# A Perceiver layer on one core: the order of ScalarE's operations bound to the order in which they are written, and four conversions spaced evenly

## The chip, the cores and the metric

The kernel runs on one core of a Trainium2 chip. A core has five engines that run side by side, each through its own queue in order: TensorE (PE in the profile; its weight loads are PEld), VectorE (DVE), ScalarE (ACT), GpSimd (POOL) and SyncE (SP), which here starts transfers. The metric is the device time of one launch in microseconds. Everything is in fp32.

## The reference

A layer of a Perceiver with 8 batches of 64 query rows of width 512 and a context of 1601 rows for each batch:

```
x = x + cross_attention(layernorm(x), context)   # 16 heads of 32, stablemax for softmax
x = x + self_attention(layernorm(x))             # 8 heads of 64, one key and value head, causal
x = x + ffn(layernorm(x))                        # 2 shared experts, and the best 2 of 8 experts

stablemax:  s = where(x >= 0, x + 1, 1 / (1 - x));  s / sum(s)
layernorm:  (x - mean) / sqrt(var + eps)
ffn experts: 512 -> 2048 -> 512, gelu between
```

The bulk of it is the projection of the 8 x 1601 context rows to keys and values, two 512 x 512 matrices.

## The kernel before

**Tiling.** The 512 query rows are four tiles of 128 (`NTT`). The context of one batch is three sections of 512 columns (24 in all) and a tail of 65 rows. Keys are kept transposed (`kT`), values by rows (`v`).

**Keys and values.** Section 0 is projected plainly (`first_keys` L383 on, `first_values`, `plain_values` L396 on): four key banks of PSUM, copied by ScalarE with the bias (L394), and one bank for each of four value products (copy in L400). From section 1 on, `products` (L337) uses a Strassen scheme: seven products of four matmuls for the keys and seven for the values of a section, in three PSUM banks that take turns (A, C, A, B, A, B, A). After product 0, 2, 3, 4 and 6 ScalarE copies the bank out (L344, or L348 twice with a bias for each half); after 1 and 5 VectorE adds. A product that takes a bank again needs the copy that reads it to be done. The sums of weight parts that the scheme needs are eight VectorE operations in `weight_parts` (L303), the differences of the context four GpSimd operations a section (L320).

**Attention.** A unit is two tiles of 128 keys of one batch, seven units a batch (the last is the tail). `score` (L504) fills four PSUM banks `ps_s` of 512 columns. `convert` (L525) turns one bank into stablemax's numerators: ScalarE writes relu(-s) (L535), relu(s) (L536) and adds 1 to the first (L537), VectorE takes the reciprocal (L538), GpSimd adds (L539) and, with every second conversion, adds to the running totals (L548, L551). The buffer `neg` is one of five. `weigh` (L555) multiplies with the values. `sums` and `finish` divide by the totals.

**First rows.** `first_rows` (L473) normalizes one tile of the queries: statistics on VectorE, `Norm.factors` (a square root on ScalarE, L258, then a reciprocal, L259, and a product, L261, on VectorE), `Norm.apply` on ScalarE (L266), four transposes on TensorE (L274) and the copy `xnT` on ScalarE (L275, in `transposed`). `q_unit` (L484) then makes the queries from all four tiles.

**Self attention.** For each pair of batches `chain` (L613) is a list of 15 steps (project, factors, apply, turn, keys, queries, scores, exps, flip, values, output, factors, apply2, rows, gate), spread over the next pair's work. Several of them end in one ScalarE operation.

**What sets the order.** The class `Plan` (L52) takes the TensorE work as units with lengths and everything else with due times, and writes the instructions in that order. A first-section product counts 3.43, a Strassen product 1.715; an attention unit of two tiles spans 11.77 of the plan's units (about 15.3 us on the chip), and its four conversions are due at 0, 0.3, 0.6 and 0.9 of it (L906). The first section's plan is: keys, first value product, the four `first_rows`, second value product, four `q_unit`, then the other value products. After writing, the framework's scheduler orders each engine's instructions itself, by what is ready and by its own costs: ScalarE's order in the kernel before is not the written one. So the four norms of the first rows stand ahead of the key copies in ScalarE's queue, though they are written after them; and at many places in the attention conversions stand ahead of a copy that is written before them.

**After the attention.** The experts follow. The first shared expert's first products (`first_hidden` L811, Gelu in L821) overlap with the last norm.

Of the kernel before, what the change touches and what calls it, by code (L numbers as in the profile page):

```python
# [1 line left out]

# [1 line left out]

# [67 lines left out]
            o[2]()  # L72


@with_exitstack
def perceiver_kernel(
    ctx: ExitStack,
# [4 lines left out]
    out,  # L82
):
    nc = tc.nc

    def pool(name, bufs, **kw):
        return ctx.enter_context(tc.tile_pool(name=name, bufs=bufs, **kw))
# [156 lines left out]
    class Norm:  # L244


        def __init__(self, tt):
            self.tt = tt
# [6 lines left out]

        def factors(self):
            self.rs = lnp.tile([P, 1], F32, name="ln_rs")
            nc.scalar.activation(self.rs, self.mv[:, 1:2], AF.Sqrt, bias=eps_t)  # L258
            nc.vector.reciprocal(self.rs, self.rs)  # L259
            self.nb = lnp.tile([P, 1], F32, name="ln_nb")  # L260
            nc.vector.scalar_tensor_tensor(  # L261
                self.nb, self.mv[:, 0:1], -1.0, self.rs, ALU.mult, ALU.mult
            )

        def apply(self, xn):
            nc.scalar.activation(  # L266
                xn, res[:, self.tt, :], AF.Identity, bias=self.nb, scale=self.rs
            )

    def transposed(dst, xn):  # L270

        pt = psx("pt").rearrange("p (c t) -> p c t", c=NC)
        for c in range(NC):
            nc.tensor.transpose(pt[:, c, :], xn[:, c * P : (c + 1) * P], ident)  # L274
        nc.scalar.copy(dst, pt)  # L275

    def cols(t):
        return t.rearrange("p (c t) -> p c t", c=NC)
# [1 line left out]
    plan = Plan()  # L280
# [56 lines left out]
    def products(i, keys):  # L337

        st = {}

        def copy(dst, src, half):

            if not keys or half is None:
                nc.scalar.copy(dst, src)  # L344
                return
            for k in range(2):
                g = 2 * half + k
                nc.scalar.activation(dst[:, k], src[:, k], AF.Identity, bias=bk_t[:, g : g + 1])  # L348

        def unit(n):  # L350
            bank, a, b = ORDER[n]
            if n == 0:
                t = w8("kT" if keys else "v")
                (kTs if keys else vs)[i] = t
                for f in range(2):
                    for r in range(2):
                        st[f, r] = t[:, 2 * f : 2 * f + 2, r * HF : (r + 1) * HF] if keys else \
                            t[:, 2 * r : 2 * r + 2, f * 256 : (f + 1) * 256]
            fresh = bank not in st
            if fresh:  # L360
                st[bank] = psa("ps_k" if keys else "ps_v").rearrange("p (k n) -> p k n", k=2)
            ps = st[bank]
            multiply(ps, (wkp if keys else wvp)[a], tparts[i][b], keys, first=fresh)
            if n == 0:
                copy(st[0, 0], ps, 0)
            elif n == 1:
                nc.vector.tensor_tensor(st[0, 0], ps, st[0, 0], ALU.add)
            elif n == 2:
                copy(st[0, 1], ps, 0)
            elif n == 3:  # L370
                copy(st[1, 1], ps, None)
            elif n == 4:
                u3 = snp.tile([P, 2, 256], F32, tag="sn", name="u3")
                copy(u3, ps, 1)
                nc.gpsimd.tensor_add(st[1, 1], st[1, 1], u3)
            elif n == 5:
                nc.vector.tensor_tensor(st[0, 1], ps, st[0, 1], ALU.add)
            else:
                copy(st[1, 0], ps, 1)

        return [lambda n=n: unit(n) for n in range(len(ORDER))]

    def first_keys():  # L383

        kTs[0] = w8("kT")
        ps = [psa("ps_k0") for _ in range(NG)]
        for c in range(NC):
            for g in range(NG):
                nc.tensor.matmul(  # L389
                    ps[g], wk[:, c, g * P : (g + 1) * P], cxs[0][:, c, :],  # L390
                    start=c == 0, stop=c == NC - 1,
                )
        for g in range(NG):
            nc.scalar.activation(kTs[0][:, g, :], ps[g], AF.Identity, bias=bk_t[:, g : g + 1])  # L394

    def plain_values(cx, dst, w):  # L396
        ps = psa("ps_v0")
        for c in range(NC):
            nc.tensor.matmul(ps[:w], cx[:, c, :], wv[:, c, :], start=c == 0, stop=c == NC - 1)  # L399
        nc.scalar.copy(dst, ps[:w])  # L400

    def first_values(t):
        if t == 0:
# [27 lines left out]
    def tail_keys(b):  # L431
        kT = tlp.tile([P, NG, 2, TAIL], F32, name="kTt")
        cx = tails[b, "x"]
        for g in range(NG):
            ps = psa("ps_kt")[:, : 2 * TAIL]
            for c in range(NC):
                nc.tensor.matmul(
                    ps, wk[:, c, g * P : (g + 1) * P], cx[:, c, :], start=c == 0, stop=c == NC - 1
                )
            for s in (slice(0, ROUND), slice(ROUND, TAIL)):  # L440
                nc.scalar.activation(
                    kT[:, g, :, s],
                    ps[:, 2 * s.start : 2 * s.stop].rearrange("p (k s) -> p k s", k=2),
                    AF.Identity, bias=bk_t[:, g : g + 1],
                )
        for k in range(2):
            tails[b + k, "k"] = kT[:, :, k, :]
# [3 lines left out]
    def tail_values(b):  # L451
        x = tails[b, "x"]
        ps = psa("ps_vt")
        for c in range(NC):
            nc.tensor.matmul(
                ps, x[:, c, 0 : 2 * ROUND], wv[:, c, :], start=c == 0, stop=c == NC - 1
            )
        for k in range(2):
            v = tails[b + k, "v"] = tlp.tile([P, E], F32, name="vt")
            nc.scalar.copy(v[:ROUND], ps[k * ROUND : (k + 1) * ROUND])  # L460
            nc.gpsimd.dma_start(out=v[ROUND:TAIL, :], in_=odd_v[b + k : b + k + 1, :])

    per = NSEC * SEC // P + 1
# [61 lines left out]
    def convert(b, u, j):  # L525

        w, n, k = tile_of(b, UNITS[u][0])[2], width(u), len(UNITS[u])
        r = j // 2
        if j % 2 == 0:
            attn[b, u, r] = at4("at")  # L530
        at = attn[b, u, r]
        pos = at[:w, (j % 2) * n : (j % 2 + 1) * n]
        ps = parts[b, u][j][:w].rearrange("p k g q -> p (k g q)")
        neg = np2("neg")[:w, :n]
        nc.scalar.activation(neg, ps, AF.Relu, scale=-1.0)  # L535
        nc.scalar.activation(pos, ps, AF.Relu)  # L536
        nc.scalar.activation(neg, neg, AF.Identity, bias=one_t[:w])  # L537
        nc.vector.reciprocal(neg, neg)  # L538
        nc.gpsimd.tensor_add(pos, pos, neg)  # L539
        if j % 2 == 0:  # L540
            return

        if u == 0 and r == 0:
            totals[b] = totp.tile([P, 2, 2, NG * SQ], F32, name="tot")
        tot = totals[b][:w, r]
        at = at[:w, : 2 * n].rearrange("p (j k c) -> p j k c", j=2, k=k)
        if u == 0:
            nc.gpsimd.tensor_add(tot, at[:, :, 0], at[:, :, 1])  # L548
        else:
            for i in range(k):  # L550
                nc.gpsimd.tensor_add(tot, tot, at[:, :, i])  # L551
# [3 lines left out]
    def weigh(b, u):  # L555
# [20 lines left out]
        if u == len(UNITS) - 1:  # L576
            acc = accs.pop(b)
            accs[b] = accp.tile([P, NG, SQ], F32, name="o_sb")
            nc.scalar.copy(accs[b], acc)

    ctT = {}

# [30 lines left out]
    def chain(tt):  # L613
# [35 lines left out]
        def keys():  # L649
# [12 lines left out]
                            skip_group_check=True,  # L662
                        )
            st["kv"] = qhp.tile([P, P], F32, name="akv")
            nc.scalar.copy(st["kv"], ps)

        def queries():
            ps = psx("ps_aq").rearrange("p (h q) -> p h q", h=H2)
# [7 lines left out]
                            skip_group_check=True,  # L676
                        )
            st["qh"] = qhp.tile([P, H2, SQ], F32, name="aqh")
            nc.scalar.mul(st["qh"], ps, float(E ** -0.5))
            st["wp"] = load_w(aWp, "awp")  # L680

        def scores():
# [22 lines left out]
        def exps():  # L705
            shape = [P, 2 * NP2, SQ]
            s = st["s"]
            nc.scalar.activation(s, s, AF.Exp)
            sm = lnp.tile([P, 2 * NP2, 1], F32, name="sm")
            nc.vector.tensor_reduce(sm, s, AX.X, ALU.add)  # L710
            nc.vector.reciprocal(sm, sm)
            nc.vector.tensor_tensor(s, s, sm.to_broadcast(shape), ALU.mult)

        def flip():
# [5 lines left out]
                        start=True, stop=True, skip_group_check=True,  # L720
                    )
            st["aT"] = sd("aT")
            nc.scalar.copy(st["aT"], pt.rearrange("p a r -> p (a r)"))

        def values():
            po = psx("po_a")
# [7 lines left out]
            st["oT"] = cols(sd("oT"))  # L734
            for half in halves:
                for j in range(2):
                    nc.scalar.copy(
                        st["oT"][j * HD2 : (j + 1) * HD2, :, half], po[half, :, j, :]
                    )

# [70 lines left out]
    def first_hidden(hc):  # L811
# [4 lines left out]
        for c in range(NC):  # L816
# [1 line left out]
                ps[:, :N0], w0[0, q][:, c, r * P : (r + 1) * P], shared_x["x"][:, c, :N0],  # L818
                start=c == 0, stop=c == NC - 1,
            )  # L820
        nc.scalar.activation(h0[q][:, r, :N0], ps[:, :N0], AF.Gelu, bias=b1_t[:, 0, hc : hc + 1])  # L821

    def first_second(hc):
        q, r = hc // QC, hc % QC
# [77 lines left out]
    for u, time in enumerate(when):  # L902
        plan.at(weighed[u], lambda u=u: weigh(*units[u]))
        plan.at(time, lambda u=u: begin(u))
        for j in range(1, 4):
            plan.at(time + 0.3 * j * wide[u] * step, lambda u=u, j=j: convert(*units[u], j))  # L906
        if u == 3 * nu:
            plan.at(time, clear)
    for tt in range(NTT):
# [614 lines left out]
```

## Time and profile before

| | us |
|---|---|
| median of 3 runs | 1389.02 |
| lowest, highest | 1387.26, 1390.02 |
| the profiled execution itself | 1385.32 |
| its span in the profile | 1383.6 |

Busy time by stages of that execution, from the table of windows:

| window (us) | TensorE | VectorE | ScalarE | GpSimd |
|---|---|---|---|---|
| 0 to 48: loads, first section | 42.56 | 19.89 | 11.09 | 23.02 |
| 48 to 150 | 102.00 | 92.63 | 67.51 | 80.54 |
| 150 to 857: attention | 695.27 | 641.33 | 445.83 | 583.10 |
| 857 to 1383.6: experts | 520.77 | 135.07 | 118.35 | 58.85 |

A row of the timeline gives start, duration, engine, line, operation, output and inputs, shapes and count, and in square brackets the idle time ahead of it with what ended it. A row of the waits gives the engine and line that waited, the engine and line that ended the wait, the sum in us, how many times, and the longest. Lines (L...) are those of the kernel before.

### The profile page before, as it was taken

The page shows a single profiled execution, that of the slowest core. Times are in us where ns is not written, and L with a number is a line of the kernel's source. Part 1 is how long each engine was busy: PE and PEld are TensorE (multiplying, and loading weights), DVE is VectorE, ACT ScalarE, POOL GpSimd, SP SyncE. Part 2 cuts the span into 40 slices and gives each one's busy share as a digit, 9 for nine tenths or more (in the row PEclk, how much of TensorE's full clock was granted, in tenths as well). Part 3 has the DMA queues.
Part 4 walks back from the last instruction along what each step waited for, and adds up shares of the span by engine and source line. Part 5 has one row for each costly group of instructions (what it writes and reads, how often), then busy time and mean ns, then how long its engine had stood idle before and what let it go on. Part 6 is the DMA issues. An engine that isn't in the chain of part 4 may idle for free.

```text
span 1383.6 us, 36463 instructions
## 1 busy us (share of the span) xinstructions
PE 1360.6 (98%) x16080; PEld 1073.2 (78%) x16080; DVE 888.9 (64%) x655; ACT 642.8 (46%) x1339; POOL 745.5 (54%) x672
## 2 busy tenths in 40 slices
PE   8999999999999999999999999999999999999998
PEld 3678788788788877778878878555786699977787
DVE  4698999988899997988988989713531000100314
ACT  3466656566666665666656766422221111122230
POOL 6288899886889986878979776600110000000020
PEclk9999999999999999999999999999999999999999
DMA  7002112112311121111111113444466267778730
GB/s 230 31 3 70 33 33 78 61 34 70 132 62 33 47 94 40 33 40 63 47 58 68 63 40 142 149 153 164 159 215 243 77 222 264 261 268 315 293 99 32
DMA packets 84804, 156.35 MB, mean 113 GB/s; under 512 B 13370, under 2 KB 14426, under 8 KB 84644
## 3 DMA queue, kind: packets, MB, share of 16 engines
q1 hardware_dynamic: 77732, 136.41, 28.3%
q0 software_dynamic: 4704, 13.91, 2.9%
q10 hardware_dynamic: 2208, 3.67, 0.9%
q8 instruction: 127, 2.08, 0.6%
q14 instruction: 33, 0.27, 0.1%
HBM read 143.24 MB, written 10.72 MB: 111 GB/s over the span
## 4 chain that ended last, share of the span: by engine, by line
PE 87%; ACT 4%; DVE 4%; POOL 3%; issue 2%; DMA 0%; DVEq 0%; POOLq 0%
PE ps_k L331 17%; PE ps_v L331 16%; PE ps_h L1367 11%; PE y L1312 6%; PE ps_s L520 4%; PE y L1321 4%; PE ps_hr L331 3%; PE ps_hh L331 3%; PE ps_o L570 3%; PE ps_h L817 3%; PE y L829 3%; DVE neg L538 3%; PE ps_v L399 1%; ACT neg L535 1%; PE ps_k L389 1%
## 5 line engine op out<-in xcount | busy, mean ns | idle before, releaser
L538 DVE RECIPROCAL neg<-neg 128x512 f32<-128x512 f32 (+1 forms) x224 | 683.8, 3091 | 57.8 <-ACT neg L537 54.6
L539 POOL TENSOR_TENSOR at<-at,neg 128x512 f32<-128x512 f32 (+1 forms) x224 | 266.6, 1195 | 126.2 <-DVE neg L538 123.2
L551 POOL TENSOR_TENSOR tot<-tot,at 128x512 f32<-128x512 f32 (+1 forms) x176 | 223.9, 1272 | 12.8
L1367 PEld LDWEIGHTS ps_h<-xgT,w1t 128*128 128x128 f32 x1024 | 147.2, 191 | 37.9 <-issue 32.7
L1372 ACT ACTIVATE hT<-ps_h,b1e 128x128 f32<-128x128 f32 (+4 forms) x128 | 50.3, 393 | 259.3 <-PE ps_h L1367 233.3
L537 ACT ACTIVATE neg<-neg,one_t 128x512 f32<-128x512 f32 (+1 forms) x224 | 162.1, 725 | 0.0
L1303 POOL DMA_DIRECT2D ys_d<-yo x12 | 6.6, 547 | 285.6 <-DVE yo L1302 285.6
L1367 PE MATMUL ps_h<-xgT,w1t 128*128 128x128 f32 (+4 forms) x1024 | 159.7, 299 | 0.0
L535 ACT ACTIVATE neg<-ps_s 128x512 f32<-128x512 f32 (+1 forms) x224 | 130.1, 583 | 62.8 <-PE ps_s L520 51.4
L331 PE MATMUL ps_k<-tx,sk 128*128 128x256 f32 x552 | 130.0, 386 | 3.8 <-ACT kT L348 3.6
L536 ACT ACTIVATE at<-ps_s 128x512 f32<-128x512 f32 (+1 forms) x224 | 131.7, 590 | 0.0
L331 PE MATMUL ps_v<-sv,tx 128*128 128x256 f32 x552 | 129.0, 384 | 1.0 <-ACT v L344 1.0
L331 PEld LDWEIGHTS ps_k<-tx,sk 128*128 128x128 f32 x552 | 101.5, 190 | 23.8 <-ACT kT L348 4.8
L331 PEld LDWEIGHTS ps_v<-sv,tx 128*128 128x128 f32 x552 | 102.4, 190 | 17.2 <-ACT v L344 1.4
L1294 DVE COPY xgT<-pt_x 128x512 f32<-128x512 f32 (+3 forms) x12 | 6.8, 592 | 141.0 <-PE pt_x L1293 141.0
L1312 PE MATMUL y<-w2t,hT 128*128 128x512 f32 x192 | 95.8, 593 | 0.0
L344 ACT COPY v<-ps_v 128x512 f32<-128x512 f32 x92 | 56.0, 608 | 75.0 <-PE ps_v L331 75.0
L348 ACT ACTIVATE kT<-ps_k,bk_t 128x256 f32<-128x256 f32 x138 | 59.5, 498 | 59.8 <-PE ps_k L331 59.8
L331 PE MATMUL ps_k<-cx,wk 128*128 128x256 f32 x368 | 86.8, 385 | 0.0
L331 PE MATMUL ps_v<-wv,cx 128*128 128x256 f32 x368 | 86.1, 383 | 0.0
L520 PEld LDWEIGHTS ps_s<-qT,kT 32*64 32x64 f32 x6144 | 69.9, 130 | 18.2 <-issue 16.8
L331 PEld LDWEIGHTS ps_k<-cx,wk 128*128 128x128 f32 x368 | 68.2, 190 | 12.8 <-issue 2.1
(263 smaller groups left out, 2013.1 us busy)
## 6 DMA issues: line engine op xcount, KB each, us to landing
w1t<-in_W_dram SPq DMA_DIRECT2D x32, 1024.0 KB, 11.5
w2t<-in_W_dram SPq DMA_DIRECT2D x32, 1024.0 KB, 12.2
cx<-in_ctxT_dram SPq DMA_DIRECT2D x23, 1024.0 KB, 5.4
w1t<-in_sW_dram SPq DMA_DIRECT2D x12, 1024.0 KB, 5.1
w2t<-in_sW_dram SPq DMA_DIRECT2D x12, 1024.0 KB, 5.6
wo<-in_woT_dram SPq DMA_DIRECT2D x4, 1024.0 KB, 5.5
awq<-in_aWq_dram SPq DMA_DIRECT2D x4, 1024.0 KB, 5.5
awp<-in_aWp_dram SPq DMA_DIRECT2D x4, 1024.0 KB, 5.6
```

Source lines behind the costliest of these rows:

```text
L331: nc.tensor.matmul(ps[:, k, :], l[:, c, k * P : (k + 1) * P], r[:, c, :], start=first and k == 0 and c == 0, stop=last and c == 1, skip_gr ...
L344: nc.scalar.copy(dst, src)
L348: nc.scalar.activation(dst[:, k], src[:, k], AF.Identity, bias=bk_t[:, g : g + 1])
L520: nc.tensor.matmul(ps[j][h, k, g, :], kT[rows, g, h], qT[rows, g, b * SQ : (b + 1) * SQ], start=True, stop=True, skip_group_check=True,)
L535: nc.scalar.activation(neg, ps, AF.Relu, scale=-1.0)
L536: nc.scalar.activation(pos, ps, AF.Relu)
L537: nc.scalar.activation(neg, neg, AF.Identity, bias=one_t[:w])
L538: nc.vector.reciprocal(neg, neg)
L539: nc.gpsimd.tensor_add(pos, pos, neg)
L551: nc.gpsimd.tensor_add(tot, tot, at[:, :, i])
L1312: nc.tensor.matmul(self.y[k], hT[:, s : s + w], w2t, start=first, stop=last)
L1367: nc.tensor.matmul(ph[:, : blk.n], w1t[:, c, f : f + P], blk.x[:, c, :], start=c == 0, stop=c == NC - 1,)
```

## The change

A class `InOrder` wraps an engine: each call through it is made under `tc.issue_after(...)` of the call before, so that the scheduler may not place it ahead of that one. `act = InOrder(tc, nc.scalar)` takes the place of `nc.scalar` for all ScalarE operations of the first rows, the products, the tails, the conversions, the self attention, the norms and the first shared expert's first Gelus. The other experts' operations, the gate's probabilities and the transfers started on ScalarE's queue are left free. Second, the four conversions of a unit are due at 0, 0.25, 0.5 and 0.75 of it. No operation is added or removed; the only new things are ordering constraints on one engine.

```diff
+class InOrder:
+    def __init__(self, tc, engine):
+        self.tc, self.engine, self.last = tc, engine, None
+
+    def __getattr__(self, name):
+        def ask(*args, **kw):
+            with self.tc.issue_after(self.last.ins) if self.last else nullcontext():
+                self.last = getattr(self.engine, name)(*args, **kw)
+            return self.last
+
+        return ask
...
+    act = InOrder(tc, nc.scalar)
...
         def factors(self):
-            nc.scalar.activation(self.rs, self.mv[:, 1:2], AF.Sqrt, bias=eps_t)
+            act.activation(self.rs, self.mv[:, 1:2], AF.Sqrt, bias=eps_t)
         def apply(self, xn):
-            nc.scalar.activation(
+            act.activation(
                 xn, res[:, self.tt, :], AF.Identity, bias=self.nb, scale=self.rs
             )
     def transposed(dst, xn):
-        nc.scalar.copy(dst, pt)
+        act.copy(dst, pt)
     def products(i, keys):
-                nc.scalar.copy(dst, src)
+                act.copy(dst, src)
-                nc.scalar.activation(dst[:, k], src[:, k], AF.Identity, bias=bk_t[:, g : g + 1])
+                act.activation(dst[:, k], src[:, k], AF.Identity, bias=bk_t[:, g : g + 1])
     def first_keys():
-            nc.scalar.activation(kTs[0][:, g, :], ps[g], AF.Identity, bias=bk_t[:, g : g + 1])
+            act.activation(kTs[0][:, g, :], ps[g], AF.Identity, bias=bk_t[:, g : g + 1])
     def plain_values(cx, dst, w):
-        nc.scalar.copy(dst, ps[:w])
+        act.copy(dst, ps[:w])
     def convert(b, u, j):
-        nc.scalar.activation(neg, ps, AF.Relu, scale=-1.0)
-        nc.scalar.activation(pos, ps, AF.Relu)
-        nc.scalar.activation(neg, neg, AF.Identity, bias=one_t[:w])
+        act.activation(neg, ps, AF.Relu, scale=-1.0)
+        act.activation(pos, ps, AF.Relu)
+        act.activation(neg, neg, AF.Identity, bias=one_t[:w])
...
-            plan.at(time + 0.3 * j * wide[u] * step, lambda u=u, j=j: convert(*units[u], j))
+            plan.at(time + 0.25 * j * wide[u] * step, lambda u=u, j=j: convert(*units[u], j))
```

The same replacement is made in `tail_keys`, `tail_values`, `weigh`, the self attention's `keys`, `queries`, `exps`, `flip`, `values`, and `first_hidden`.

More of the change, by code (lines that the diff above doesn't have):

```diff
@@ L1 @@
-from contextlib import ExitStack
+from contextlib import ExitStack, nullcontext
 import numpy as np
@@ L440, in tail_keys @@
             for s in (slice(0, ROUND), slice(ROUND, TAIL)):
-                nc.scalar.activation(
+                act.activation(
                     kT[:, g, :, s],
@@ L459, in tail_values @@
             v = tails[b + k, "v"] = tlp.tile([P, E], F32, name="vt")
-            nc.scalar.copy(v[:ROUND], ps[k * ROUND : (k + 1) * ROUND])
+            act.copy(v[:ROUND], ps[k * ROUND : (k + 1) * ROUND])
             nc.gpsimd.dma_start(out=v[ROUND:TAIL, :], in_=odd_v[b + k : b + k + 1, :])
@@ L578, in weigh @@
             accs[b] = accp.tile([P, NG, SQ], F32, name="o_sb")
-            nc.scalar.copy(accs[b], acc)
+            act.copy(accs[b], acc)
     ctT = {}
@@ L664, in keys @@
             st["kv"] = qhp.tile([P, P], F32, name="akv")
-            nc.scalar.copy(st["kv"], ps)
+            act.copy(st["kv"], ps)
         def queries():
@@ L678, in queries @@
             st["qh"] = qhp.tile([P, H2, SQ], F32, name="aqh")
-            nc.scalar.mul(st["qh"], ps, float(E ** -0.5))
+            act.mul(st["qh"], ps, float(E ** -0.5))
             st["wp"] = load_w(aWp, "awp")
@@ L707, in exps @@
             s = st["s"]
-            nc.scalar.activation(s, s, AF.Exp)
+            act.activation(s, s, AF.Exp)
             sm = lnp.tile([P, 2 * NP2, 1], F32, name="sm")
@@ L722, in flip @@
             st["aT"] = sd("aT")
-            nc.scalar.copy(st["aT"], pt.rearrange("p a r -> p (a r)"))
+            act.copy(st["aT"], pt.rearrange("p a r -> p (a r)"))
         def values():
@@ L736, in values @@
                 for j in range(2):
-                    nc.scalar.copy(
+                    act.copy(
                         st["oT"][j * HD2 : (j + 1) * HD2, :, half], po[half, :, j, :]
@@ L820, in first_hidden @@
             )
-        nc.scalar.activation(h0[q][:, r, :N0], ps[:, :N0], AF.Gelu, bias=b1_t[:, 0, hc : hc + 1])
+        act.activation(h0[q][:, r, :N0], ps[:, :N0], AF.Gelu, bias=b1_t[:, 0, hc : hc + 1])
     def first_second(hc):
```

## The prediction

> **What bounds the kernel now.** I read the page's busy times first.
>
> ```profile
> PE 1360.6 (98%) x16080; PEld 1073.2 (78%) x16080; DVE 888.9 (64%) x655; ACT 642.8 (46%) x1339; POOL 745.5 (54%) x672
> ```
>
> TensorE works 98% of the span, so only its pauses can be won back, and every new pause is paid. By stages (the table of windows), the attention runs from about 48 to 857 us; in 50 to 850 us VectorE is busy 91% and GpSimd 82%. ScalarE is half idle throughout, so the question is not how much it does but when.
>
> Next, what TensorE waited for in 48 to 860 us (the view of waits; us in total, times, longest), ScalarE's part of it:
>
> ```profile
> PE ps_k L331 <- ACT kT L348: 3.6, 5, 1.2
> PE ps_v L331 <- ACT v L344: 2.4, 3, 1.0
> PE ps_v L331 <- ACT u L344: 2.2, 2, 1.6
> PE ps_k L331 <- ACT u L348: 0.9, 1, 0.9
> ```
>
> The sum is 9.1 us: a product of four matmuls needs the bank that ScalarE's copy of an earlier product has not yet freed. The same waits read from the weight loads sum to 15.2 us, partly hidden behind the matmul in flight. Counting by how much the start-to-start distance of matmuls exceeds its usual step, I find 14 such places and 11.6 us. That is all that the attention can gain. Its cause is seen at one of them (the timeline):
>
> ```profile
> 711.61 0.81 ACT L266 ACTIVATE xn_a<-res,ln_nb,ln_rs 128x512 f32<-128x512 f32 x1 [0.53 <-DVE ln_nb L261]
> 712.33 0.58 ACT L535 ACTIVATE neg<-ps_s 128x512 f32<-128x512 f32 x1
> ...
> 714.85 0.85 ACT L348 ACTIVATE kT<-ps_k,bk_t 128x256 f32<-128x256 f32 x2
> 715.85 2.40 PE L331 MATMUL ps_k<-tx,sk 128*128 128x256 f32 x10 [0.77 <-ACT kT L348]
> ```
>
> A norm held ScalarE while VectorE made its factor, then two conversions (six operations) ran ahead of the copy, and TensorE waited for that.
>
> The start is different: there the order is loose, to the kernel's profit (timeline, ScalarE and TensorE):
>
> ```profile
> 20.64 1.52 ACT L266 ACTIVATE xn<-res,ln_nb,ln_rs 128x512 f32<-128x512 f32 x2 [3.51 <-DVE ln_nb L261]
> 21.64 3.60 PE L399 MATMUL ps_v<-wv,cx 128*128 128x512 f32 x8
> 22.06 0.46 ACT L258 ACTIVATE ln_rs<-ln_mv,eps_t 128x1 f32<-128x1 f32 x2
> ...
> 22.86 0.81 ACT L266 ACTIVATE xn<-res,ln_nb,ln_rs 128x512 f32<-128x512 f32 x1 [0.33 <-DVE ln_nb L261]
> ...
> 24.81 2.40 ACT L394 ACTIVATE kT<-ps_k,bk_t 128x512 f32<-128x512 f32 x4
> 25.07 1.91 PE L274 MATMUL pt<-ident,xn 128*128 128x128 f32 x16
> 26.82 3.60 PE L399 MATMUL ps_v<-wv,cx 128*128 128x512 f32 x8
> 27.09 0.60 ACT L400 COPY v<-ps_v 128x512 f32<-128x512 f32 x1
> 27.56 2.08 ACT L275 COPY xnT<-pt 128x512 f32<-128x512 f32 x4
> 30.25 13.90 PE L487 MATMUL ps_q<-xnT,wq 128*128 128x512 f32 x32
> ```
>
> All four norms were done beside the key and value products, before the key copies; so the 16 transposes ran in one go of 1.91 us and TensorE did not pause.
>
> **The change, part by part.**
>
> *Binding at the start: a loss.* The scheduled order of the changed kernel binds ScalarE to: four key copies, the first value copy, then for each of the four row tiles square root, application, copy of the transposes. TensorE's order stays keys, first values, 16 transposes, second values, queries; it therefore stands still while ScalarE goes through the tiles one by one. Working: the first value product ends at 21.64 + 3.60 = 25.24; its copy takes 0.60 to 25.87; the switch to the table of the square root takes 1.28, to 27.15. Before, that switch lay at 8.65 us, under the load of the weights. Then one tile: square root to end of application is 22.06 to 23.67 = 1.61 (VectorE's reciprocal and factor are inside), hand-over to TensorE 0.1, four transposes 0.60 (another tile's row), copy 0.59 and the next square root behind it: 2.90. The last transposes end at 27.15 + 3 x 2.90 + 1.61 + 0.70 = 38.2, against 25.07 + 1.91 = 27.0 before: 11.2 us. One such factor took 1.13 instead of 0.25 us beside GpSimd's addition; GpSimd now has its four context differences and the row additions in this stretch, so I add 0.8: **+12.0**. [...] Nothing absorbs it later: in 48 to 150 us TensorE was busy 102.00 of 102.00 us. VectorE's eight weight sums stand ahead of the first reciprocal in its queue; at 0.68 us each (GpSimd idle, as it is by then) they end at about 25.8, just in time; at the 1.75 they took beside GpSimd they would add up to 7.
>
> [...]
>
> ```profile
> 906.19 0.29 ACT L258 ACTIVATE ln_rs<-ln_mv,eps_t 128x1 f32<-128x1 f32 x1 [5.80 <-DVE ln_mv L254]
> 906.50 1.28 ACT L821 ACT_TABLE_LOAD   x1
> 907.80 0.58 ACT L821 ACTIVATE hTq<-ps_h,b_t 128x384 f32<-128x384 f32 x1
> ```
>
> The load begins 0.02 us after the operation before it ends, and the next follows at once. [...]
>
> *TensorE's clock at the start: a loss, perhaps.* [...] In the changed kernel it has only four bursts of transposes in 13 us. The trace shows a cold start but no such pause: the first 12 matmul records took 7.78 us, where the steady pace (9 in 4.03) makes about 5.4: 2.4 us lost, while the granted clock in the page reads full throughout. [...]
>
> *Binding and even spacing in the attention: a gain.* Bound, ScalarE's order has one conversion between two copies. A conversion takes 1.58 us of ScalarE start to start, a product 1.725 of TensorE: it fits, so copies come on time. The square root and the application of a norm stand some ten operations apart, so VectorE's factor (0.4 us) is ready. Spaced at quarters, a unit of 15.3 us gives VectorE one reciprocal (3.09 us) each 3.8 us instead of a gap and then two close together (0.9 and the next unit's 0). That takes away the stalls. What it may add: an operation that waits now blocks all copies behind it. Such waits are the conversion for its buffer (GpSimd's addition freed it late 8 times, 10.9 us in all, in before) and the exponential for VectorE's scaled scores (3.9 us, twice); behind them stand the copy of the next product, then TensorE. In between a table load and a square root between a conversion and a copy overfill a slot by about 0.9 us, at some of four norms. Of 11.6 I let 2 stay or come back: **-9.5**, between -11.6 and, if the blocking is worse than now, +2.
>
> *The first shared expert's Gelu's, bound from 857 us on:* TensorE had no wait for ScalarE of weight there, ScalarE was busy 118 of 526 us; one table load more, hidden by that idleness. Nothing; if the last norm held a Gelu back, 1 to 2 us.
>
> **Sum.** Span 1383.6 + 12.0 + 1.5 - 9.5 = 1387.6 us. The profiled execution itself took 1385.32, and the median of the runs is 1389.02, 3.7 above it; the difference is carried over: 1389.0 + 4.0 = **1393.0 us**.
>
> **Rivals.**
>
> *Even (about 1389.7).* Clock stays full as the row says, start +11, gain -10.3. For it: the granted-clock row; against it: the cold start seen at 5.4 us.
>
> *Much slower (about 1401).* One order for all makes ScalarE wait at conversions. VectorE at 91% falls behind, buffers (five) come free late, and each copy behind them is late: the gain turns to nothing, +12 to +14. For it: the 10.9 us of buffer waits, and that a free order could go round them. Against it: ScalarE's queue was in order in before too, only the order was another.
>
> *Faster (about 1385.5).* The tile loop at the start costs far less than I think. It decides from a start delay under 8.8 us, that is a loop below 2.2 us per tile, with all 11.6 won back. Against it: square root to application is 1.61 on the trace and transposes and copy 1.1 more. Only overlap of these could do it, and the order forbids it.
>
> *The change does nothing in the attention* (spacing and order end up as before): then the start alone, 1401 to 1403; included with the second rival.
>
> **How the numbers follow.** A difference under 0.2% (2.8 us) is not told from none here. Main case 0.50, of which 0.07 comes out below +2.8; even 0.18; much slower 0.23; faster 0.09. So slower 0.43 + 0.23 = 0.66, same 0.25, faster 0.09. The main case alone spans 1391 to 1397. The range runs from 1386.5 (start 9.7, no cold clock, all won: -1.9, less some of the 2.8 us by which the runs shown differ) to 1402 (start 13, nothing won back), leaving out most of the faster case and the worst of the slower one.
>
> **What would show it.** In the timeline of 25 to 42 us: transposes in four groups some 2.9 us apart, each released by ScalarE's application; second value product from about 38 instead of 26.8, queries from about 42 instead of 30.25; matmuls after them spread wider for some us if the clock fell. In the waits of 60 to 870 us: ScalarE's lines for ps_k and ps_v together from 9.1 down to 1 to 2; VectorE's waiting for L537 in shorter pieces. The prediction is wrong if the transposes come sooner than 36 or later than 41 us, or if TensorE's idle in the attention does not fall.

## The result

The changed kernel takes 1400.78 us (median of 6 runs, 1399.68 to 1401.68), the kernel before 1388.88 us beside it (6 runs): a ratio of 1.0079 (95% interval 1.0067 to 1.0091), **11.9 us slower**. The forecast was slower by 4.0, with a range of 1386.5 to 1402; 1400.8 lies near its upper end.

The page of the changed kernel, its busy times and the row of the granted clock:

```profile
PE 1368.7 (98%) x16080; PEld 1081.3 (77%) x16080; DVE 882.9 (63%) x655; ACT 654.1 (47%) x1340; POOL 744.8 (53%) x672
PEclk9899999999999999999999999999999999999999
```

TensorE is busy for about the same share, and the clock row has one 8 in its second slice where before there were only nines. The loss arises in that neighbourhood. TensorE's timeline there (start and duration in us, engine, line, operation, tiles, count, and in brackets the idle time ahead and what ended it):

```profile
21.58 3.60 PE L416 MATMUL ps_v<-wv,cx 128*128 128x512 f32 x8
28.79 0.63 PE L291 MATMUL pt<-ident,xn 128*128 128x128 f32 x4 [3.61 <-ACT xn L84]
32.13 1.11 PE L291 MATMUL pt<-ident,xn 128*128 128x128 f32 x4 [2.72 <-ACT xn L84]
35.92 1.11 PE L291 MATMUL pt<-ident,xn 128*128 128x128 f32 x4 [2.67 <-ACT xn L84]
39.14 1.11 PE L291 MATMUL pt<-ident,xn 128*128 128x128 f32 x4 [2.11 <-ACT xn L84]
40.05 5.64 PE L416 MATMUL ps_v<-wv,cx 128*128 128x512 f32 x8
45.52 13.90 PE L504 MATMUL ps_q<-xnT,wq 128*128 128x512 f32 x32
```

The transposes come in four groups, each released by ScalarE's application (L84 is the line of the wrapper, which now stands for all of them). The second value product begins at 40.05 instead of 26.82 and takes 5.64 instead of 3.60; the queries begin at 45.52 instead of 30.25, **15.27 us later**. ScalarE over the same time:

```profile
25.21 0.58 ACT L84 COPY v<-ps_v 128x512 f32<-128x512 f32 x1 [2.75 <-PE ps_v L416]
25.81 1.28 ACT L84 ACT_TABLE_LOAD   x1
27.11 0.29 ACT L84 ACTIVATE ln_rs<-ln_mv,eps_t 128x1 f32<-128x1 f32 x1
27.83 0.81 ACT L84 ACTIVATE xn<-res,ln_nb,ln_rs 128x512 f32<-128x512 f32 x1 [0.42 <-DVE ln_nb L278]
29.45 0.58 ACT L84 COPY xnT<-pt 128x512 f32<-128x512 f32 x1 [0.81 <-PE pt L291]
29.93 0.30 ACT L84 ACTIVATE ln_rs<-ln_mv,eps_t 128x1 f32<-128x1 f32 x1
31.26 0.81 ACT L84 ACTIVATE xn<-res,ln_nb,ln_rs 128x512 f32<-128x512 f32 x1 [1.03 <-DVE ln_nb L278]
```

Copy, table load, square root, application: no gap at the table load. Two of the four factors were late (0.99 and 1.03 instead of 0.42 us). The table of windows (us, then busy times with counts of TensorE, its weight loads, VectorE, ScalarE and GpSimd, granted clock, share of the DMA engines, GB/s) shows the clock:

```profile
30.00:40.10 10.10, 3.19 (x13) 2.39 (x14) 2.32 (x7) 4.23 (x9) 8.31 (x7) 0.52 0.00 1
40.10:45.50 5.40, 5.40 (x9) 2.18 (x9) 0.00 (x0) 0.58 (x1) 0.33 (x1) 0.63 0.00 0
45.50:59.00 13.50, 13.50 (x33) 6.06 (x32) 2.25 (x3) 0.59 (x1) 0.00 (x0) 1.00 0.00 1
```

While TensorE does only four bursts of transposes, its clock is granted at about half (0.52), and it stays there for some four of the 5.4 us of full work that follow (0.63 on the mean).

In the attention the waits of TensorE that the change was to remove are gone. The view of waits, 60 to 872 us:

```profile
PE ps_s L537 <- issue: 2.4, 1, 2.4
PE ps_s L537 <- DVE s_a L714: 1.5, 1, 1.5
PE ps_akv L677 <- issue: 1.0, 1, 1.0
PE ps_s L537 <- DVE v L384: 0.5, 1, 0.5
PE ps_k L348 <- issue: 0.4, 1, 0.4
```

No line of ScalarE is left; its four lines had 9.1 us. But two waits are new or longer: the first line stands near 293 us, the second near 772. The lateness, that is the start of a matmul in the changed kernel less the start of the same matmul in the kernel before, is 15.27 us at 107, 12.49 at 280, 15.58 at 309, 12.97 at 381, 8.33 at 760, 12.14 at 786 and 11.13 at 864 us. So some 11.8 us were won back, about what was counted before (11.6), but 3.1 were lost near 293 us, 3.8 near 772 us and about 0.8 near 580 us: **net 4.1** of the expected 9.5.

In the profiled executions the spans differ by 14.8, more than the medians' 11.9. The execution of the kernel before that was profiled had run 3.6 us under its median. Of the extra lateness 1.6 us arise near 1082 us, in the experts, where the two kernels do the same. TensorE does not pause there, but it runs eight matmuls of only 10 rows in 3.7 us, and behind them the clock is granted at half in the changed kernel (0.50) and not in the profile of the kernel before (1.00; windows, the changed kernel first):

```profile
1081.80:1085.20 3.40, 3.40 (x9) 2.46 (x8) 0.37 (x1) 0.33 (x1) 0.00 (x0) 0.50 0.00 0
1068.40:1071.80 3.40, 3.40 (x12) 1.97 (x11) 2.07 (x3) 0.00 (x0) 0.00 (x0) 1.00 0.00 0
```

The same eight matmuls take 3.69 us in both. With nothing bound the clock varies as well: executions of the kernel before have a mean granted clock of 0.996 (span 1387.2 us) to 1.000 (1383.6). So this part of the difference need not be the change's doing.

### The profile page after: what moved, and what is told of

Read it like the earlier page. It is cut to its first block, busy times and chain, and to the rows that moved or that the text cites. A ratio compares the mean times of both kernels' runs of the same rounds, so it can differ in the third digit from the quotient of the medians.

```text
span 1398.4 us, 36373 instructions
## 1 busy us (share of the span) xinstructions
PE 1368.7 (98%) x16080; PEld 1081.3 (77%) x16080; DVE 882.9 (63%) x655; ACT 654.1 (47%) x1340; POOL 744.8 (53%) x672
## 4 chain that ended last, share of the span: by engine, by line
PE 96%; DMA 2%; DVE 1%; ACT 1%; issue 1%; DVEq 0%
PE ps_v L348 21%; PE ps_k L348 21%; PE ps_h L1384 11%; PE y L1329 6%; PE ps_s L537 6%; PE y L1338 4%; PE ps_o L587 4%; PE ps_hr L348 3%; PE ps_hh L348 3%; PE ps_h L834 3%; PE y L846 3%; DMA cx<-in_ctxT_dram 1%; PE ps_v L416 1%; PE ps_aq L690 1%; PE ps_kt L454 1%; PE ps_vt L472 1%
## 5 line engine op out<-in xcount | busy, mean ns | idle before, releaser
L84 ACT ACTIVATE neg<-ps_s 128x512 f32<-128x512 f32 (+1 forms) x224 | 127.7, 570 | 66.2 <-PE ps_s L537 64.3
L84 ACT ACTIVATE neg<-neg,one_t 128x512 f32<-128x512 f32 (+1 forms) x224 | 157.5, 703 | 0.0
L84 ACT ACTIVATE at<-ps_s 128x512 f32<-128x512 f32 (+1 forms) x224 | 128.1, 572 | 0.0
L84 ACT COPY v<-ps_v 128x512 f32<-128x512 f32 x96 | 56.4, 587 | 116.0 <-PE ps_v L348 89.7
L84 ACT ACTIVATE kT<-ps_k,bk_t 128x256 f32<-128x256 f32 (+1 forms) x142 | 60.7, 479 | 73.8 <-PE ps_k L348 64.3
L537 PE MATMUL ps_s<-qT,kT 32*64 32x64 f32 x6144 | 78.1, 232 | 4.3 <-issue 2.4
```

The lines of the kernel that those rows point to most:

```text
L84: self.last = getattr(self.engine, name)(*args, **kw)
L537: nc.tensor.matmul(ps[j][h, k, g, :], kT[rows, g, h], qT[rows, g, b * SQ : (b + 1) * SQ], start=True, stop=True, skip_group_check=True,)
```

## The experiments

**The start's binding alone.** The kernel before, with only the first section's operations bound (key and value copies, norms of the first rows, their transposes' copies):

```diff
+    act = InOrder(tc, nc.scalar)
...
     def first_keys():
-            nc.scalar.activation(kTs[0][:, g, :], ps[g], AF.Identity, bias=bk_t[:, g : g + 1])
+            act.activation(kTs[0][:, g, :], ps[g], AF.Identity, bias=bk_t[:, g : g + 1])
...
     def first_rows(tt):
-        norm = Norm(tt)
+        norm = Norm(tt, act)
```

> Only the first section's ScalarE operations (key copies, value copies, the four norms of the first rows and their copies) are bound; attention, self attention and spacing stay as before. Theory A (the start alone loses, the attention gains about 4): the query product starts near 45.5 instead of 30.3 us and nothing later gives it back: +15 us, about 1404. Rival B (the binding in the attention is what costs; the start's pause is given back by later waits): +0 to +6, 1389 to 1395.

Measured: 1402.4 us against 1387.36, ratio 1.0104 (1.0085 to 1.0123), +15.0 us. In its trace the lateness is 14.9 at 109 us and 14.4 at 930: what the start loses is not given back, but for 0.5, and TensorE's waits for ScalarE in the attention are those of the kernel before to the digit. Theory A holds.

**All but the start.** The changed kernel, with the first section's operations left free:

```diff
-        norm = Norm(tt)
+        norm = Norm(tt, nc.scalar)
...
-            act.activation(kTs[0][:, g, :], ps[g], AF.Identity, bias=bk_t[:, g : g + 1])
+            nc.scalar.activation(kTs[0][:, g, :], ps[g], AF.Identity, bias=bk_t[:, g : g + 1])
```

> The changed kernel with the first section's ScalarE operations left free; binding and even spacing in the attention stay. Theory A: the start is as before, the attention keeps its gain of about 4 (11 won, some 7 lost at new pauses near 293 and 772 us of the changed kernel): 1384 to 1386. If those two pauses came from the shifted timing and not from the order, 1378 to 1381. Rival B: 1395 or more.

Measured: 1382.35 us against 1387.36, ratio 0.9964 (0.9956 to 0.9973), -5.0 us. That is a little better than expected, and faster than both kernels. The two pauses are there again (2.8 us near 278, 1.5 near 758), so they belong to the new order of the attention and not to the shift in time.

**Even spacing alone.**

```diff
-            plan.at(time + 0.3 * j * wide[u] * step, lambda u=u, j=j: convert(*units[u], j))
+            plan.at(time + 0.25 * j * wide[u] * step, lambda u=u, j=j: convert(*units[u], j))
```

> The kernel before with the conversions at 0, 0.25, 0.5 and 0.75, nothing bound. Theory A1 (the conversions' bunching, 0.9 followed by 0, is what puts them ahead of the copies): TensorE's waits for ScalarE's copies fall by half, -3 to -6 us, 1383 to 1386. Theory A2 (only the order that the scheduler gives matters): within 1 us of before.

Measured: 1387.32 against 1387.36 us, ratio 0.9998 (0.9989 to 1.0006): nothing. The waits:

```profile
PE ps_k L331 <- ACT kT L348: 2.9, 4, 1.2
PE ps_v L331 <- ACT u L344: 2.2, 2, 1.6
PE ps_v L331 <- ACT v L344: 2.2, 3, 1.0
```

They fell from 9.1 to 8.2 us with the fourth line's unchanged 0.9. By the names of its tiles, ScalarE's order in this trace is that of the kernel before in all but two of its 1339 operations: left free, the scheduler makes the same order whether the plan spaces the conversions by 0.3 or by 0.25. So the new spacing hardly reached the engine here, and A1 falls.

**Binding alone.** The changed kernel with 0.3 in place of 0.25.

> The changed kernel with the old spacing of 0, 0.3, 0.6, 0.9: binding alone. Theory A2 (order alone removes the waits): as the changed kernel, 1400 to 1402. Theory A1 (even spacing is needed too): some of TensorE's waits for copies come back, 1403 to 1407.

Measured: 1405.84 against 1387.36 us, ratio 1.0129 (1.0112 to 1.0147), +18.5, against +15.0 for the start alone. So A2 falls as well: with the old spacing the binding in the attention costs about 3.4 us, with even spacing it wins 3 to 5. Each part is worth nothing or less by itself. The waits show how:

```profile
PE ps_v L348 <- DVE v L384: 1.8, 1, 1.8
PE ps_s L537 <- DVE v L384: 1.3, 1, 1.3
PE ps_s L537 <- ACT at L84: 1.0, 1, 1.0
...
PE ps_sum L608 <- POOL tot L568: 0.7, 1, 0.7
```

ScalarE's copies are on time here too, but VectorE's additions and GpSimd's totals come late. In ScalarE's queue two conversions stand back to back at 32 places instead of 21, as the old spacing has them (0.9 of one unit and 0 of the next); that this makes the others late is argued, not tested. The pause near 293 us is here as well (2.7 us), the one near 772 is not: that one needs binding and spacing together.

**The first norms written first.** All bound, but the norms are written ahead of the keys, as the free order had them:

```diff
+            for tt in range(NTT):
+                plan.add(0.0, lambda tt=tt: first_norm(tt))
             plan.add(4 * FULL, first_keys)
```

> The changed kernel, everything bound, but the statistics, factors and applications of the four first norms are written ahead of the first keys; only the written order differs. If the start's loss comes from the written order of the norms, not from binding as such: 16 transposes in one go at about 25 us, queries from about 30, total as with the free start, 1381 to 1385. If binding itself costs at the start (waits of a bound queue for the rows' transfers at 13 to 21 us): key copies late, 1386 or more.

Measured: 1389.07 against 1387.87 us, ratio 1.0010 (1.0002 to 1.0017); 10.7 us of the change's loss are gone, but it stays 6.2 us behind the free start. ScalarE's timeline:

```profile
20.98 0.81 ACT L84 ACTIVATE xn<-res,ln_nb,ln_rs 128x512 f32<-128x512 f32 x1 [6.57 <-DVE ln_nb L278]
23.20 0.81 ACT L84 ACTIVATE xn<-res,ln_nb,ln_rs 128x512 f32<-128x512 f32 x1 [1.22 <-DVE ln_nb L278]
28.33 2.40 ACT L84 ACTIVATE kT<-ps_k,bk_t 128x512 f32<-128x512 f32 x4
```

One square root and one application after the other wait for VectorE (1.2 us each), where the free order had paired them, so the key copies begin at 28.33 instead of 24.81. TensorE pauses 2.88 us for them among its transposes, its clock falls to 0.66 in 30 to 35 us, and the queries are 5.2 us late. So the written order is most of the start's loss. The rest is a bound queue that waits for VectorE, and of its 5.2 us the half clock behind the pause takes 1.8 (the second value product lasts 5.40 instead of 3.60).

**The clock at the start.** The changed kernel with extra matmuls in the pauses, nine 128x512 whose result nobody reads, so that the pauses stay but not the idleness:

```diff
+    def warm(n):
+        ps = psa("ps_w")
+        for k in range(n):
+            nc.tensor.matmul(ps, cxs[0][:, 0, 0:P], wv[:, 0, :], start=True, stop=True)
...
+        warm(3 if tt == 0 else 2)
         transposed(first_rows.x[:, :, tt * P : (tt + 1) * P], xn)
```

> The changed kernel with nine extra matmuls (128x512) in TensorE's pauses of the start, whose result nobody reads: three ahead of the first transposes, two ahead of each other four. The pauses between the bursts of transposes stay, TensorE's idleness goes. If the granted clock, about 0.5 from 30 to 44 us, is what makes the start 15 instead of 11 us: clock 1.0 there, second value product back to 3.6 us, transposes 0.6, queries from about 42 instead of 45.5, 1396 to 1398. If the clock row is only a reading and the delay is ScalarE's chain alone: 1400 to 1402.

Measured: 1392.3 against 1387.87 us, ratio 1.0035 (1.0023 to 1.0047): 7 to 8 us faster than the change with nine matmuls more. At the start it is as expected:

```profile
38.33 0.66 PE L291 MATMUL pt<-ident,xn 128*128 128x128 f32 x4 [0.39 <-ACT xn L84]
38.82 3.60 PE L416 MATMUL ps_v<-wv,cx 128*128 128x512 f32 x8
42.26 13.90 PE L510 MATMUL ps_q<-xnT,wq 128*128 128x512 f32 x32
```

and in the windows of the same kernel

```profile
30.00:38.80 8.80, 6.00 (x22) 2.61 (x21) 2.69 (x7) 4.00 (x7) 7.47 (x7) 1.00 0.00 1
38.80:42.30 3.50, 3.50 (x11) 1.59 (x10) 0.00 (x0) 0.59 (x1) 0.82 (x1) 1.00 0.02 5
```

Clock full, queries 12.0 us late instead of 15.27: **about 3.3 us of the start were the clock, 12.0 the chain of ScalarE.** The parting holds to some 0.4 us: this execution was already 0.36 us ahead at the first value product (21.22 against 21.58), and on the other hand one factor of VectorE came 0.46 us later in it (1.45 against 0.99). The remaining gain was not expected: the pause near 293 us is missing in this trace. The next experiment is about that.

**The pause near 293 us.** In the changed kernel TensorE stops within a group of scores for which no engine is named, and the clock falls after it (TensorE's timeline, then SyncE's, then the windows):

```profile
289.55 1.24 PE L537 MATMUL ps_s<-qT,kT 32*64 32x64 f32 x94
293.16 0.79 PE L537 MATMUL ps_s<-qT,kT 32*64 32x64 f32 x34 [2.37 <-issue]
293.88 3.38 PE L348 MATMUL ps_v<-sv,tx 128*128 128x256 f32 x8
```

```profile
284.97 0.37 SPq L151 DMA_DIRECT2D awq<-in_aWq_dram  x1
285.39 0.50 SPq L653 DMA_DIRECT2D awkv<-in_aWk_dram  x1
285.94 0.50 SPq L653 DMA_DIRECT2D awkv<-in_aWv_dram  x1
286.55 0.79 SPq L658 DMA_DIRECT2D abp_t<-in_abp_dram  x1
```

```profile
290.50:293.10 2.60, 0.29 (x27) 0.15 (x16) 1.84 (x1) 0.00 (x0) 0.90 (x2) 1.00 0.45 117
293.10:297.00 3.90, 3.84 (x42) 3.16 (x43) 1.34 (x1) 1.69 (x3) 3.11 (x3) 0.56 0.02 4
```

The eight matmuls after it take 3.38 us where eight such take 1.99. The same place had a pause of 0.91 us before, with no fall of the clock:

```profile
279.19 0.57 PE L520 MATMUL ps_s<-qT,kT 32*64 32x64 f32 x35 [0.91 <-issue]
```

What changed is SyncE's order: before, the loads of key and value weights and bias (0.5 MB) went out at 223 us and only the 1 MB of query weights at 272; bound, all four go out together, right ahead of the scores. A 16 KB packet of the instruction queue (a DMA queue of its own, which the page lists as "q8 instruction") starts 0.1 us ahead of these scores in the kernel before, 1.15 us after their start in the changed one. The experiment takes the free start and asks for the 0.5 MB with the output weights, earlier:

```diff
         def start():
             st["wo"] = load_w(woT, "wo")
+            st["wkv"] = cols(sd("awkv"))
+            for k, src in enumerate((aWk, aWv)):
+                nc.sync.dma_start(...)
+            abp_t = st["abp"] = sd("abp_t")
+            nc.sync.dma_start(out=abp_t, in_=abp.partition_broadcast(P))
...
         def apply():
-            st["wkv"] = cols(sd("awkv"))
-            ...
+            abp_t = st.pop("abp")
```

> The free start with even spacing and binding, but the self attention's loads of the key and value weights and of the bias are started with the load of the output weights, well ahead, instead of right behind the 1 MB of the query weights. If TensorE's pause of 2.8 us near 278 us and the half clock after it come from its instructions being fetched behind those 0.5 MB: that pause falls to about 1.1 us as in the kernel before and the clock stays full there: -3 us against the free start, 1378 to 1380. If the pause is tied to the order of scores and banks: unchanged, 1382 to 1383.

Measured: **1378.5 us** against 1387.87, ratio 0.9931 (0.9916 to 0.9946): the fastest, 9.4 us under the kernel before. The pause is now

```profile
274.62 1.24 PE L537 MATMUL ps_s<-qT,kT 32*64 32x64 f32 x94
277.24 0.56 PE L537 MATMUL ps_s<-qT,kT 32*64 32x64 f32 x34 [1.37 <-issue]
277.73 1.99 PE L348 MATMUL ps_v<-sv,tx 128*128 128x256 f32 x8
```

and the clock stays at 1.00. Set side by side, the instruction packet starts -0.1, 0.23 and 1.39 us after the scores (before, this one, free start alone), and TensorE's idle time is 0.91, 1.37 and 2.77 us; it goes on 2.2 to 2.6 us after the packet's start in all three. So the pause follows the packet, and moving the weights moved the packet. The other traces fit: where the packet starts within about 0.1 us of these scores, the pause is 1.0 to 1.3 us (spacing alone, start alone, the last experiment below), and where it starts 1.26 and 1.27 us after them, 2.7 and 2.5 us (binding alone, norms first). The weights are not all that sets it: in the kernel with extra matmuls the same four loads go out at 282 us, as far ahead of the scores as in the changed kernel (4.6 us), yet the packet starts 2.1 us ahead of them and they run through without a pause; why was not tested. That instructions are what TensorE waits for is not written in any row; it is the reading that fits all ten traces at this place. A packet's start alone does not mark a pause: in the changed kernel 15 other groups of scores have one within 1.6 us of their start and run through.

**The pause near 772 us.** In the changed kernel (timeline, all engines):

```profile
765.78 6.56 DVE L555 RECIPROCAL neg<-neg 128x512 f32<-128x512 f32 x2 [4.05 <-ACT neg L84]
...
772.26 0.69 DVE L714 TENSOR_TENSOR s_a<-ps_as,mask 128x256 f32<-128x256 f32 x2
...
772.68 1.15 PE L537 MATMUL ps_s<-qT,kT 32*64 32x64 f32 x32 [1.47 <-DVE s_a L714]
```

The fourth bank for the scores is held by the self attention's scores, which VectorE takes up only after two reciprocals. In 775 to 778 us the clock is 0.50. An instruction packet is not what holds this one: with the extra matmuls it starts 1.95 us ahead of the scores, and the pause is the same 1.5 us. The last experiment writes that step later, on top of the one above:

```diff
-            (scores, 1), (exps, 2), (flip, 2), (values, 1),
+            (scores, 1.8), (exps, 1.2), (flip, 2), (values, 1),
```

> The kernel with free start and earlier loads, and the self attention's scores written 4 of the plan's units later (step 1.8 instead of 1, the exponential's 1.2 instead of 2). If the pause of 1.5 us near 755 us (scores of the cross attention waiting for a bank that VectorE's scaling of the self attention's scores frees only behind two reciprocals) costs its own length and the half clock behind it: both go, -3.5 us, about 1375. If VectorE is simply late there and the wait moves elsewhere: 1378 to 1379.

Measured: 1381.97 against 1390.72 us, ratio 0.9938 (0.9924 to 0.9952), -8.7 us: no better than without it (0.9931), and not the 1375 of the first theory. The pause at 755 us and the half clock are gone (the place cost 5.3 us in the lateness of the kernel above, now nothing), but TensorE waits 1.1 us for VectorE ahead of the self attention's transposes in an earlier round, stops 1.3 us at 544 us with no engine named, and loses another 1.4 us near 788 us. What was taken away here came back there.

## Why the prediction was right, and where its sizes were not

*Direction and its reason: right.* The start loses, the attention gains, the start is larger. Start alone +15.0, everything else -5.0. The signs that were named came: the last transposes end at 40.25 us (36 to 41 was the bound), and TensorE's listed waits in the attention fall from 11.4 to 5.8 us.

*That the range held is partly luck.* The main case spanned 1391 to 1397 and was missed. The range's upper end stood for a start of 13 us with nothing won back; what came is a start of 15.3 us with 4.1 won back. Two terms were too small against the change, the clock by 1.8 and the attention's losses by 5.4, and a wide range covered their sum.

*The start's chain: right.* Forecast 12.0 (11.2 for the chain, 0.8 for VectorE beside GpSimd); measured 12.0 with the clock held up. Second value product and queries were forecast for about 38 and 42 us; with the clock held up they were found at 38.8 and 42.3, in the changed kernel itself at 40.05 and 45.52. The table load took 1.28 us with 0.02 us to either neighbour, as the row had it. Within the chain a group came 3.2 to 3.8 us after the last, not 2.9, the late factors included. One slip in the working changes nothing: at 712 us five operations, not six, ran ahead of the copy. The start of 9.7 us at the lower end of the range no run shows: with the clock held up it was 12.0.

*The clock: direction right, size halved.* The sum takes 1.5 for it, a term that no run shows; it cost about 3.3 (15.27 against 12.0): 2.0 on the value product, the rest on three bursts of transposes at 1.11 instead of 0.63 and what waited for them. The row of the page, which read full throughout, was no evidence against a loss: the trace of the kernel before has no clock record ahead of 10.26 us, and the row shows full speed where nothing is recorded (1.00 in the window of 5 to 10.26 us). The matmuls themselves start 0.85 us apart until 9.8 us and 0.43 us apart from 10.5 us on.

*The attention: the step that failed.* -9.5 was made of 11.6 to be won and 2 that would stay or come back. Won were 11.8, but 7.7 came back. I looked for new waits in ScalarE's queue, which is what the change binds, and there were almost none. They came from two engines that it does not name: SyncE, whose loads the new order pushed together, and VectorE, whose scaling stands behind two reciprocals. Each brought a second payment, the half clock behind the pause, larger than the pause's own part that was new: near 293 us 1.5 for the longer pause and 1.6 for the clock, near 772 us 1.5 and 2.3. (That a late packet of instructions makes the first of these pauses is a reading; that the earlier loads halve it and keep the clock up is measured.) The prediction had a cold clock only at the start, and it did not weigh the pause of 0.91 us that the kernel before already had at this place.

*Even spacing: credited by argument only.* I held the binding for the cause and the spacing for a help. Alone, the spacing gives nothing, since a free scheduler undoes it, and the binding loses 3.4; only together do they win.

*The rival "much slower"* (1401) had the right number by another way: there copies were to be late behind conversions. Copies were on time, and conversions waited for GpSimd less than before (1.5 us of ScalarE's waits in the attention instead of 10.9).

## What to carry to other kernels

Before binding a queue to its written order, read where the free order differed to the kernel's profit: here four norms written late but run early were worth 15 us at the start, and binding all but them turned a loss of 11.9 into a gain of 5. Price a new pause of TensorE twice, for its length and for a fall of the clock behind it (here 3.3 us at the start, 1.6 and 2.3 in the attention, none behind the 1.37 us at 277 us), and measure the second by filling the pause with matmuls whose result nobody reads. After any change of order, look at what SyncE sends together: here 0.5 MB of loads sent earlier took TensorE's idle time at a place where no engine is named from 2.77 to 1.37 us.

## What the runs showed of the hardware

The granted clock fell to about half in three places of the changed kernel beside the start: 0.56 after the pause of 2.4 us near 293, 0.50 after the 1.5 us near 772, and 0.50 from 1081.8 us after no pause at all. The pause near 772 us brings a fall in the kernel with extra matmuls at the start too (0.53 in 767 to 770 us), and with the earlier loads the seven 128x256 matmuls timed behind it, from 757.04 us, take 3.35 us, where eight such take 1.99 from 745.85 us. But 1.37 us of idleness within scores (277 us, earlier loads) and 1.61 us among the products of the kernel before (155.7 us) left it at 1.00. So the length of a pause alone does not decide; what does, no run here shows.

In the windows of the changed kernel's trace the clock is at 0.50 from 30.5 to 44.1 us at the start, then from 293.3 to 296.7, from 774.6 to 778.0 and from 1081.8 to 1085.2 us, and at 1.00 for 3 us on either side of each.

A 16 KB packet of the instruction queue that started 1.5 us later, behind weight transfers, went with a pause of 2.77 instead of 0.91 us within TensorE's small score matmuls. That they outran the supply of their instructions is the reading given above, not a row of the profile.
